# Three experts' first layers as 15 transposed products each, on a four-layer convolutional mixer

## The chip, the core and the metric

The kernel runs on one core of one Trainium2 chip. Its metric is the device time of one execution in microseconds (us): the median of several runs, with the lowest and the highest beside it. All data are 4-byte floats.

[...]

## The reference

The input `x` has 8 images of 384 channels and 32 x 32 pixels. Four layers follow, each `x = x + layer(_gn(x))`, where `_gn` is a group norm over 32 groups. The first is attention behind depthwise convolutions, the third a 7x7 depthwise convolution, the fourth a mixture of branches. The change touches the second, a mixture of four experts that all see every pixel:

```python
def _L1_conv_ref(x, gate_w, gate_b, w1, b1, w2, b2):
    ...
    scores = jax.nn.softmax(x_flat @ gate_w + gate_b, -1)
    top_v, top_i = jax.lax.top_k(scores, K)
    top_w = jax.nn.softmax(top_v, -1)
    wmap = top_w.T.reshape(K, b, h, w)
    present = (top_i[:, :, None] == jnp.arange(e)[None, None, :]).any(0)
    coef = jnp.einsum('ke,kbhw->ebhw', present.astype(x.dtype), wmap)
    hdn = jax.nn.relu(jnp.einsum('bchw,edc->ebdhw', x, w1) + b1[:, None, :, None, None])
    y = jnp.einsum('ebdhw,eod->ebohw', hdn, w2) + b2[:, None, :, None, None]
    out = jnp.einsum('ebohw,ebhw->bohw', y, coef)
    return out
```

`present` asks only whether any pixel chose an expert in a place. Where every expert is chosen somewhere in both places, `coef` is 1 everywhere, and the layer is the plain sum of four two-layer networks with 384 hidden units. The kernel computes that sum, records the gate logits beside it, and repeats from there by another path if some expert was never chosen.

## The kernel before, in words

Channels lie on the 128 partitions in three blocks (`NC` = 3); an image is 1024 pixels in the free dimension. The experts' stage, in the function `experts`, goes through the 8 images in order, each in two halves of 512 pixels (`HF`), and a half has two parts. The engines PE, ACT, DVE and POOL keep the order in which the program issues their work here (`manual_schedule`); SP's order is set by a scheduler.

First layers: for each of four experts `e` and three blocks `dc` of hidden units, three matmuls of 128 x 128 weights with 512 columns add up in one PSUM tile `ph` (line 1306), and ACT writes `relu(ph + b1)` into `hs` (line 1310). `hs` is one buffer of [block, expert, 512].

Second layers: the product of the 3 x 3 blocks of `w2` with the 3 x 2 blocks of `hs` (the half is cut again into two quarters of 256 pixels, `QF`) is made with 15 block products in place of 18. The table `PRODUCTS` gives for each which sum of weight blocks (`wsum`, made once by POOL), which sum of hidden blocks (`hs_sum`) and to which output blocks it is added or subtracted. The four experts add up in PSUM, so one product is four matmuls of 256 columns into a tile `p` (line 1217; four such tiles), and DVE adds each to its two or more places in the residual tile `r` (lines 1231 and 1233). The hidden sums (`HSUMS`, `sums`, line 1210) are made by DVE: eight for the first three experts in one operation each, eight for the fourth, and two more, for all four experts, in the middle of the products.

Between these run, by place in the loop: `normed` (ACT: the normed input `xn` of the next half, four buffers; issued at product 2), `residual` (loads of the next image's `zraw` and `x`, and the DVE sums `add_x`, line 1115; issued during the first layers), `logits` (24 small matmuls, an ACT copy and two transposes, in the first layers of an image's second half), and `next_layer`, the norm of the finished image for the third layer: `moments2` (DVE), `over_groups` (14 small matmul records, `gn_ps`), `norm2` (DVE with one power on POOL), and for each block `pass_on` (ACT scale, a DVE transpose, two POOL copies of edge rows, a store from SP). These ran after the first, third and following groups of the next image's first layers:

```python
if h == 0 and passing and k in (0, 2, 3, 4, 5, 6):
    next(passing)
...
if h == 1 and k == 3 and b + 1 < B:
    next(ahead)
if k == 9:
    sums(hs, HSUMS[:-2], slice(0, E - 1))
```

## Time and profile before

| What | Value |
|---|---|
| median of 3 runs | 3170.65 us (3167.68 to 3175.04) |
| the profiled execution's own time | 3172.27 us |
| its span in the profile | 3170.5 us |
| mean granted PE clock | 0.982 |
| experts' stage: first `ph` matmul to last `r` operation | 1731.2 to 2669 us |
| `ph` matmul records, `p` matmul records | 1152, 1920 |
| DVE `hs_sum` operations | 288 |
| POOL busy over the whole span | 253.9 us (8%) |

Times in a timeline are microseconds from the span's start: the start of a line's first operation, then the time until the last of its merged operations ends. In brackets stands the idle time of that engine before it, and what ended that. In the groups a line carries engine, operation, output and inputs with shapes, the count, the busy time and the mean of one in ns. Matmuls overlap in the pipeline, so one takes longer than the distance to the next.

### The profile page before, as it was taken

The numbers are of one execution on the slowest core, as the hardware profiler recorded it, in microseconds if no ns is written. First come the engines' busy times: TensorE is split into PE (matmuls) and PEld (weight loads), VectorE is DVE, ScalarE is ACT, GpSimd is POOL, SyncE is SP. The second block draws the span as 40 slices with busy tenths as digits, with TensorE's granted clock in tenths as the row PEclk, the third lists the DMA queues.
The fourth block names the chain that finished last, engine by engine and source line by source line (L and its number), as shares of the span: only waits on it lengthen the run. The fifth ranks groups of instructions, "written<-read, shape, count | busy, mean of one in ns | idle before, by whom it ended". The sixth has DMA issues, their size and how long they took to land.

```text
span 3170.5 us, 42235 instructions
## 1 busy us (share of the span) xinstructions
PE 3023.9 (95%) x17740; PEld 1605.6 (51%) x17740; DVE 1694.7 (53%) x2570; ACT 1190.1 (38%) x1356; POOL 253.9 (8%) x415
## 2 busy tenths in 40 slices
PE   4988999999999999999998999999999999886998
PEld 3775434343433334343433576676665666555543
DVE  6998354445444444445445464564554555447164
ACT  3554453535445353535442221212212112446510
POOL 2432000000000000000001100000000000111400
PEclk9999999999999999999999999999999999998999
DMA  6787011011101111011004021121121113867775
GB/s 222 270 280 288 33 41 65 23 62 43 60 25 60 43 43 62 23 62 43 11 25 163 20 64 40 64 64 40 64 64 49 42 44 129 332 223 241 234 226 185
DMA packets 89089, 322.84 MB, mean 102 GB/s; under 512 B 13608, under 2 KB 16000, under 8 KB 84664
## 3 DMA queue, kind: packets, MB, share of 16 engines
q1 hardware_dynamic: 64936, 251.71, 23.5%
q10 hardware_dynamic: 13776, 35.82, 3.6%
q0 software_dynamic: 10176, 32.51, 3.0%
q8 instruction: 141, 2.31, 0.3%
q14 instruction: 60, 0.49, 0.1%
HBM read 211.66 MB, written 111.68 MB: 102 GB/s over the span
## 4 chain that ended last, share of the span: by engine, by line
PE 82%; DVE 8%; DMA 6%; issue 2%; ACT 1%; POOL 1%; SPq 0%; ACTq 0%; POOLq 0%; DVEq 0%
PE ph L1306 16%; PE sc L734 15%; PE av L753 14%; PE p L1217 13%; PE sc L632 7%; PE sc L687 4%; PE sc L809 4%; DMA w<-in_w 3%; DVE stats L213 2%; DVE y L462 2%; PE ps L1783 2%; PE po L2197 1%; PE po L2200 1%; PE po L2208 1%; DVE xt L429 1%
## 5 line engine op out<-in xcount | busy, mean ns | idle before, releaser
L741 ACT ACTIVATE e<-sc 128x1024 f32<-128x1024 f32 x512 | 483.2, 1031 | 608.2 <-PE sc L734 608.1
L1306 PE MATMUL ph<-xn,w 128*128 128x512 f32 x1152 | 504.1, 596 | 3.0 <-ACT xn L315 3.0
L734 PE MATMUL sc<-qT,kT 64*128 64x512 f32 x2048 | 473.9, 602 | 0.0
L753 PE MATMUL av<-e,vT 128*64 128x512 f32 x2048 | 467.8, 599 | 0.0
L1310 ACT ACTIVATE hs<-ph,b 128x512 f32<-128x512 f32 x192 | 131.8, 686 | 705.7 <-PE ph L1306 705.4
L1306 PEld LDWEIGHTS ph<-xn,w 128*128 128x128 f32 x1152 | 218.2, 191 | 264.6 <-issue 258.6
L734 PEld LDWEIGHTS sc<-qT,kT 64*128 64x128 f32 x2048 | 186.9, 186 | 282.0 <-issue 231.1
L753 PEld LDWEIGHTS av<-e,vT 128*64 128x64 f32 x2048 | 135.6, 137 | 316.4 <-issue 316.4
L632 PE MATMUL sc<-y,pw 128*128 128x512 f32 x576 | 249.3, 594 | 0.0
L491 PE MATMUL ps<-xt,wx 64*64 64x256 f32 x3456 | 200.3, 392 | 35.2 <-DVE xt L429 20.1
L1231 DVE TENSOR_TENSOR r<-r,p 128x256 f32<-128x256 f32 x416 | 157.1, 417 | 138.9 <-PE p L1217 138.9
L769 DVE LOAD_MASK_SELECT sm<-av x64 | 0.9, 14 | 417.0 <-PE av L753 417.0
L771 DVE RECIPROCAL inv<-sm 128x512 f32<-128x512 f32 x64 | 214.6, 3353 | 2.2
L491 PEld LDWEIGHTS ps<-xt,wx 64*64 64x64 f32 x3456 | 158.8, 139 | 75.6 <-issue 38.9
L1065 PE MATMUL ps<-xt,wx 64*64 64x256 f32 (+1 forms) x2912 | 159.1, 377 | 22.6 <-ACT wx L1539 11.8
L632 PEld LDWEIGHTS sc<-y,pw 128*128 128x128 f32 x576 | 109.1, 190 | 139.7 <-issue 138.3
L1217 PE MATMUL p<-hs_sum,wsum 128*128 128x256 f32 x768 | 173.6, 379 | 0.0
L1217 PEld LDWEIGHTS p<-hs_sum,wsum 128*128 128x128 f32 x768 | 146.3, 190 | 19.5
L1210 DVE TENSOR_TENSOR hs_sum<-hs,hs_sum 128x768 f32<-128x768 f32 (+1 forms) x192 | 146.9, 779 | 4.9
L1065 PEld LDWEIGHTS ps<-xt,wx 64*64 64x64 f32 x2912 | 109.1, 138 | 70.8 <-ACT wx L1539 14.1
L687 PE MATMUL sc<-pw_v,y 128*128 128x384 f32 x384 | 128.2, 495 | 10.9 <-ACT y L315 10.9
L366 ACT COPY o<-ps 128x2048 f32<-128x2048 f32 x56 | 103.9, 1856 | 81.6 <-PE ps L491 47.4
(320 smaller groups left out, 3246.8 us busy)
## 6 DMA issues: line engine op xcount, KB each, us to landing
raw<-y SPq DMA_DIRECT2D x72, 512.0 KB
y<-raw SPq DMA_DIRECT2D x24, 1536.0 KB
x<-x SPq DMA_DIRECT2D x23, 608.0 KB
xt<-x SPq DMA_DIRECT2D x23, 608.0 KB
w<-in_w ACTq DMA_DIRECT2D x36, 384.0 KB
xn<-in_x SPq DMA_DIRECT2D x24, 512.0 KB
x<-in_x SPq DMA_DIRECT2D x16, 768.0 KB
z<-z POOLq DMA_DIRECT2D x16, 768.0 KB, 4.3
```

The source lines that it names most:

```text
L491: nc.tensor.matmul(ps[64 * d : 64 * d + 64, 2 * i + e, cc], lhsT=w[r, 12 * cc + 6 * e + 3 * d + k, :], rhs=xt0s[ct][r, 16 * d + 4 * u + 2 ...
L632: nc.tensor.matmul(ps[:, h, :], lhsT=w[:, ct, pair, :], rhs=y[:, ct, h * HF : (h + 1) * HF], start=ct == 0, stop=ct == NC - 1,)
L687: nc.tensor.matmul(ps[:, m, :C], lhsT=y[:, ct, (m0 + m) * P : (m0 + m + 1) * P], rhs=pw_v[:, ct, :], start=ct == 0, stop=ct == NC - 1,)
L734: nc.tensor.matmul(sc[:, s, :], lhsT=kTs[b][r, pair, m * P : (m + 1) * P], rhs=qTs[b][r, pair, h * HF : (h + 1) * HF], start=True, stop=True,)
L741: nc.scalar.activation(e, sc, AF.Exp, scale=1.0 if shifted else HD**-0.5)
L753: nc.tensor.matmul(av[64 * s : 64 * s + 64, :], lhsT=vTs[0][:, m, c0 : c0 + 64], rhs=e[:, s, :], start=m == 0, stop=m == N // P - 1,)
L771: nc.vector.reciprocal(inv, sm)
L1065: nc.tensor.matmul(ps[64 * d : 64 * d + 64, 2 * i + e, c % 2, images], lhsT=w[r, d * K7 + k, :], rhs=by_slot(xts[ct])[r, 16 * d + column(c ...
L1210: nc.vector.tensor_add(rows_of(o, hs, s), rows_of(i, hs, s), rows_of(j, hs, s))
L1217: nc.tensor.matmul(ps[:, :QF], lhsT=block(w)[:, e], rhs=rows_of(x, hs, e), start=e == 0, stop=e == E - 1,)
L1231: nc.vector.tensor_tensor(out=o, in0=o, in1=ps[:, :QF], op=op)
L1306: nc.tensor.matmul(ph, lhsT=w1[:, e, ct, dc * P : (dc + 1) * P], rhs=xns[b, h][:, ct, :], start=ct == 0, stop=ct == NC - 1,)
```

## The change

In all halves but the first, three of the four experts make their first layer as `w1` blocks times input by the same scheme of 15 products, transposed: what were sums of results become sums of inputs, and the reverse. POOL makes twelve sums of normed input blocks (`FORMS`, tile `forms`) for each half, shared by the three experts, and once the weight sums `w1sum`. Each product is a single matmul of 256 columns into a `p` tile (`dual`); ACT and DVE merge it at once into the hidden blocks through ten intermediate nodes, which lie in the fourth expert's part of `hs_sum`: per expert 2 ACT copies, 19 DVE operations and 3 ReLUs in place (`rectify`). The fourth expert keeps its three groups of matmuls, one ahead of each of the others (`classical`). The sums for the second layers move from DVE to POOL, one expert at a time. `next_layer`, the next image's loads and `add_x` move from the first layers to between the second layers' products (`jobs`); `xn` has two buffers.

```diff
+FORMS = (
+    (4, (1, 1), (0, 1), -1),
+    (14, 4, (2, 1), 1),
...
+DUAL = (
+    (14, ((14, "p14"),)),
+    (4, (((1, 1), "p4", 14, 1),)),
+    (13, ((1, "p13", 14, 1),)),
+    (1, (((1, 0), "p1", 1, 1),)),
+    (12, ((9, "p12", 1, 1),)),
+    (0, (((0, 0), "p0", 9, 1),)),
+    (11, ((6, "p11", 9, 1),)),
+    (3, (((0, 1), "p3", 6, 1),)),
+    (7, ((10, 6, "p7", -1),)),
+    (10, ((11, "p10"), ((0, 0), (0, 0), "p10", 1))),
+    (9, ((8, 11, "p9", -1), ((1, 0), (1, 0), 8, 1))),
+    (8, ((3, "p8", 8, 1), ((1, 1), (1, 1), 3, 1), (10, 10, 3, 1))),
+    (2, (((2, 0), "p2", 10, 1),)),
+    (6, (((0, 1), (0, 1), "p6", 1), ((2, 1), "p6", 10, 1))),
+    (5, (((1, 1), (1, 1), "p5", 1), ((2, 1), (2, 1), "p5", 1))),
+)
+NODE_AT = {n: i for i, n in enumerate((1, 9, 6, 10, 14, 11, 8, 3))}
+READY = {6: (0,), 5: (1, 2)}
...
-                xn = xns[b, h] = wq.tile([P, NC, HF], FP, tag="xn", name="xn", bufs=4)
+                xn = xns[b, h] = wq.tile([P, NC, HF], FP, tag="xn", name="xn", bufs=2)
...
+            forms = wq.tile([P, len(FORMS), QF], FP, name="forms")
+            w1sum = wq.tile([P, len(wslot) - 2, R15, P], FP, name="w1sum")
...
+            def make_forms(xn):
+                for o, i, j, sign in FORMS:
+                    i, j = (form_of(v, xn) for v in (i, j))
+                    nc.gpsimd.tensor_tensor(
+                        out=forms[:, fslot[o]], in0=i, in1=j,
+                        op=ALU.add if sign > 0 else ALU.subtract,
+                    )
+
+            def rectify(hs, e, m):
+                affine(hs[:, m, e], hs[:, m, e], 1.0, b1[:, e, m : m + 1], AF.Relu)
+
+            def dual(hs, e, xn):
...
+                for n, ops in DUAL:
+                    ps = got[f"p{n}"] = ep.tile([P, HF], FP, tag="p", name="p")
+                    nc.tensor.matmul(
+                        ps[:, :QF], lhsT=block1(PRODUCTS[n][0])[:, e], rhs=form_of(n, xn),
+                        start=True, stop=True,
+                    )
+                    for o, i, *more in ops:
+                        if not more:
+                            nc.scalar.copy(at(o), at(i))
+                            continue
+                        j, sign = more
+                        nc.vector.tensor_tensor(
+                            out=at(o), in0=at(i), in1=at(j), op=ALU.add if sign > 0 else ALU.subtract
+                        )
+                    for m in READY.get(n, ()):
+                        rectify(hs, e, m)
...
-            def sums(hs, some, s):
+            def sums(hs, some, s, eng=nc.vector):
...
+                    nxt = (b, 1) if h == 0 else (b + 1, 0)
+                    if i == 2 and nxt[0] < B:
+                        normed(*nxt)
...
-                        sums(hs, HSUMS[-2:], slice(0, E))
+                        sums(hs, HSUMS[-2:], slice(0, E), nc.gpsimd)
+                    if i == 4 and nxt[0] < B:
+                        make_forms(xns[nxt])
+                    for job in jobs.get(i, ()):
+                        job()
...
+                    next(gating, None)
+                    for e in range(R15):
+                        classical(hs, R15, e, xn)
+                        dual(hs, e, xn)
                         next(gating, None)
+                        if e == R15 - 1:
+                            sums(hs, HSUMS[:-2], slice(R15, E), nc.gpsimd)
+                        sums(hs, HSUMS[:-2], slice(e, e + 1), nc.gpsimd)
...
+                jobs = {}
+                if h == 0:
+                    if passing:
+                        for i in (0, 1, 2, 5, 7, 9):
+                            jobs[i] = (lambda p=passing: next(p),)
+                    if b + 1 < B:
+                        jobs[10] = (lambda b=b: fetch_next(b + 1),)
+                elif b + 1 < B:
+                    jobs[0] = (lambda b=b: next(ahead[b + 1]),)
+                products(b, h, hs, jobs)
```

More of the change, by code (lines that the diff above doesn't have):

```diff
@@ L112 @@
 )
+R15 = 3
+FORMS = (
+    (4, (1, 1), (0, 1), -1),
+    (14, 4, (2, 1), 1),
+    (13, (2, 0), 14, -1),
+    (1, (0, 0), (1, 0), -1),
+    (0, (0, 0), (2, 0), -1),
+    (11, (0, 1), (2, 0), -1),
+    (3, (2, 1), (0, 1), -1),
+    (10, (1, 0), 14, -1),
+    (8, (0, 1), (1, 0), -1),
+    (2, (0, 0), (0, 1), -1),
+    (6, (2, 1), (2, 0), -1),
+    (5, (1, 1), (1, 0), -1),
+)
+PLAIN = {7: (0, 1), 9: (1, 0), 12: (2, 0)}
+DUAL = (
[15 rows of a table added]
+)
+NODE_AT = {n: i for i, n in enumerate((1, 9, 6, 10, 14, 11, 8, 3))}
+READY = {6: (0,), 5: (1, 2)}
 def img(a):
@@ L1187, in experts @@
             hs_sum = ew.tile([P, len(HSUMS) - 2, E, QF], FP, name="hs_sum")
+            fslot = {n: i for i, (n, *_) in enumerate(FORMS)}
             lg = ew.tile([P, NT, E], FP, name="lg")
@@ L1198, in experts, with block1, sum_weights @@
                 )
+            w1slot = {n: i for i, n in enumerate(n for n in wslot if n not in (8, 9))}
+            def block1(n):
+                n = {8: (1, 1), 9: (2, 0)}.get(n, n)
+                if isinstance(n, tuple):
+                    return w1[:, :R15, n[0], n[1] * P : (n[1] + 1) * P]
+                return w1sum[:, w1slot[n]]
+            def sum_weights():
+                for o, i, sign, j in WSUMS:
+                    first8 = o == 8 and i != 8
+                    nc.gpsimd.tensor_tensor(
+                        out=block1(5 if first8 else o), in0=block1(5 if i == 8 else i), in1=block1(j),
+                        op=ALU.add if sign > 0 else ALU.subtract,
+                    )
@@ new lines, in form_of @@
+            def form_of(n, xn):
+                n = PLAIN.get(n, n) if isinstance(n, int) else n
+                if isinstance(n, tuple):
+                    return xn[:, n[0], n[1] * QF : (n[1] + 1) * QF]
+                return forms[:, fslot[n]]
+            def make_forms(xn):
+                for o, i, j, sign in FORMS:
+                    i, j = (form_of(v, xn) for v in (i, j))
+                    nc.gpsimd.tensor_tensor(
+                        out=forms[:, fslot[o]], in0=i, in1=j,
+                        op=ALU.add if sign > 0 else ALU.subtract,
+                    )
@@ new lines, in rectify, with at @@
+            def rectify(hs, e, m):
+                affine(hs[:, m, e], hs[:, m, e], 1.0, b1[:, e, m : m + 1], AF.Relu)
+            def dual(hs, e, xn):
+                got = {}
+                def at(n):
+                    if isinstance(n, str):
+                        return got[n][:, :QF]
+                    if isinstance(n, tuple):
+                        return hs[:, n[0], e, n[1] * QF : (n[1] + 1) * QF]
+                    return hs_sum[:, NODE_AT[n], E - 1]
+                for n, ops in DUAL:
[3 more added lines that the diff above has]
+                        start=True, stop=True,
+                    )
+                    for o, i, *more in ops:
[5 more added lines that the diff above has]
+                            out=at(o), in0=at(i), in1=at(j), op=ALU.add if sign > 0 else ALU.subtract
+                        )
+                    for m in READY.get(n, ()):
+                        rectify(hs, e, m)
@@ L1199, in experts, with classical @@
+            def classical(hs, e, dc, xn):
+                ph = eh.tile([P, HF], FP, tag="h", name="ph", bufs=3)
+                for ct in range(NC):
+                    nc.tensor.matmul(
+                        ph, lhsT=w1[:, e, ct, dc * P : (dc + 1) * P], rhs=xn[:, ct, :],
+                        start=ct == 0, stop=ct == NC - 1,
+                    )
+                nc.scalar.activation(hs[:, dc, e], ph, AF.Relu, bias=b1[:, e, dc : dc + 1])
             nc.vector.tensor_reduce(badd, b2, AX.X, ALU.add)
@@ L1206, in rows_of, with products @@
                 return hs_sum[:, hslot[n], s]
-            def sums(hs, some, s):
+            def sums(hs, some, s, eng=nc.vector):
                 for o, i, j in some:
-                    nc.vector.tensor_add(rows_of(o, hs, s), rows_of(i, hs, s), rows_of(j, hs, s))
-            def products(b, h, hs):
+                    eng.tensor_add(rows_of(o, hs, s), rows_of(i, hs, s), rows_of(j, hs, s))
+            def products(b, h, hs, jobs):
                 r, begun = rs[b], set()
@@ L1220, in products @@
                         )
-                    if i == 2:
-                        if h == 0:
-                            normed(b, 1)
-                        elif b + 1 < B:
-                            normed(b + 1, 0)
+                    nxt = (b, 1) if h == 0 else (b + 1, 0)
+                    if i == 2 and nxt[0] < B:
+                        normed(*nxt)
                     for sign, m, n in outs:
@@ L1297, in logits, with fetch_next @@
                 yield
-            ahead, passing = None, None
+            ahead, passing = {}, None
+            def fetch_next(b):
+                ahead[b] = residual(b)
+                next(ahead[b])
             for b, h in product(range(B), range(2)):
                 hs = ew.tile([P, NC, E, HF], FP, tag="hs", name="hs")
-                gating = logits(b)
-                for k, (e, dc) in enumerate(TODO):
-                    ph = eh.tile([P, HF], FP, tag="h", name="ph", bufs=3)
-                    for ct in range(NC):
-                        nc.tensor.matmul(
-                            ph, lhsT=w1[:, e, ct, dc * P : (dc + 1) * P], rhs=xns[b, h][:, ct, :],
-                            start=ct == 0, stop=ct == NC - 1,
-                        )
-                    nc.scalar.activation(hs[:, dc, e], ph, AF.Relu, bias=b1[:, e, dc : dc + 1])
-                    if h == 0 and passing and k in (0, 2, 3, 4, 5, 6):
-                        next(passing)
-                    if h == 0 and k == 9 and b + 1 < B:
-                        ahead = residual(b + 1)
-                        next(ahead)
-                    if h == 1 and k in (0, 1, 2, 4):
-                        next(gating, None)
-                    if h == 1 and k == 3 and b + 1 < B:
-                        next(ahead)
-                    if k == 9:
-                        sums(hs, HSUMS[:-2], slice(0, E - 1))
-                sums(hs, HSUMS[:-2], slice(E - 1, E))
+                xn = xns[b, h]
+                gating = logits(b) if h else iter(())
+                if (b, h) == (0, 0):
+                    for k, (e, dc) in enumerate(TODO):
+                        classical(hs, e, dc, xn)
+                        if k == 9:
+                            sums(hs, HSUMS[:-2], slice(0, E - 1))
+                    sums(hs, HSUMS[:-2], slice(E - 1, E))
+                    sum_weights()
+                else:
+                    next(gating, None)
+                    for e in range(R15):
+                        classical(hs, R15, e, xn)
+                        dual(hs, e, xn)
+                        next(gating, None)
+                        if e == R15 - 1:
+                            sums(hs, HSUMS[:-2], slice(R15, E), nc.gpsimd)
+                        sums(hs, HSUMS[:-2], slice(e, e + 1), nc.gpsimd)
                 if (b, h) == (B - 1, 1):
@@ L1325, in experts @@
                     begin_layer2(B - 1, er)
-                products(b, h, hs)
+                jobs = {}
[8 more added lines that the diff above has]
+                products(b, h, hs, jobs)
                 if h == 1:
```

## The prediction, made before the changed kernel ran

> **What bounds the kernel now.** I read the page first: busy shares, then the chain that ended last. TensorE is busy 95% of the span and the chain lies on it for 82%; the two lines to be changed, `ph` (first layers) and `p` (second layers), hold 16% and 13%.

> ```profile
> PE 3023.9 (95%) x17740; PEld 1605.6 (51%) x17740; DVE 1694.7 (53%) x2570; ACT 1190.1 (38%) x1356; POOL 253.9 (8%) x415
> PE 82%; DVE 8%; DMA 6%; issue 2%; ACT 1%; POOL 1%; SPq 0%; ACTq 0%; POOLq 0%; DVEq 0%
> ```

> Then the timeline of one half image, for prices. A 4-byte matmul shows as two records. From 2099.62 to 2115.07 are 36 records, 0.429 each: 0.859 per matmul of 512 columns. The next 24 take 5.18 to 2120.25: 0.431 per matmul of 256. TensorE stops nowhere: half an image is 36 x 0.859 + 60 x 0.431 = 56.8, plus 1.5 for gate logits or 1.9 for the norm's group matmuls; sixteen halves make 936, and the stage runs from 1731.2 to 2667.9.

> ```profile
> 2099.62 15.61 PE L1306 MATMUL ph<-xn,w 128*128 128x512 f32 x36
> 2115.07 5.34 PE L1217 MATMUL p<-hs,w 128*128 128x256 f32 x24
> 2117.12 2.14 DVE L1210 TENSOR_TENSOR hs_sum<-hs,hs_sum 128x256 f32<-128x256 f32 x5
> 2120.25 3.62 PE L1217 MATMUL p<-hs,wsum 128*128 128x256 f32 x16
> 2133.88 1.80 DVE L1231 TENSOR_TENSOR r<-r,p 128x256 f32<-128x256 f32 x5
> ```

> VectorE: independent 256-element operations follow each other every 0.345 ((1.80-0.42)/4); one that needs the last takes about 0.45. So everything the change adds on other engines is free only while TensorE need not wait, and I look for those waits.

> **The saving.** In 15 of 16 halves (the first stays), three experts' 27 wide matmuls (23.2) become 45 narrow ones (19.4): 3.8 less per half, **57.0** in all. The bound from below is the same figure: no other TensorE work goes.

> **(a) The tail of the transposed products.** Each expert needs 19 vector operations for 15 products of 0.431. For the first eight operations VectorE keeps step. The last six products carry eleven. The ninth product's operation ends 4.5 after the expert's first matmul started (9 x 0.431, 0.2 until it can be read, 0.42); eight more at 0.40 bring block (0,1), and a ReLU over 512 elements (0.80, the mean of the group `xn<-r,tb,s`) makes it 8.5. PE ends the last expert at 6.47 and, after experts 0 and 1 of product P0, wants that block at 7.33: with the hand-overs a wait of 1.4, and nothing else to run. Three of the eleven read two SBUF tiles; the next view says what GpSimd does to them.

> ```profile
> 1738.32 1.26 POOL L1196 TENSOR_TENSOR wsum<-w 128x512 f32<-128x512 f32 x1 [4.87 <-DMA r<-z]
> 1738.42 1.18 DVE L1200 TENSOR_TENSOR badd<-badd,zn_t 128x3 f32<-128x3 f32 x1
> 1739.52 0.17 DVE L1201 TENSOR_TENSOR ref<-gm,gmy 128x24 f32<-128x24 f32 x1
> 2657.52 0.75 DVE L1231 TENSOR_TENSOR r<-r,p 128x256 f32<-128x256 f32 x2 [1.30 <-PE p L1217]
> 2657.57 0.75 POOL L1522 TENSOR_TENSOR w<-w 128x84 f32<-128x84 f32 x2 [0.60 <-PE p L1217]
> ```

> A three-element sum took 1.18, not 0.17: it ended with the GpSimd sum beside it. The two `r<-r,p` beside GpSimd lost nothing; one of their inputs is in PSUM. So only the three operations with two SBUF inputs should wait, each for up to one GpSimd operation. GpSimd then is in sums all through the last expert. Its 256-element sum is in no row; bounds are 0.397 (84 elements) and 1.263 (512), linear between them 0.745. Three waits add 2.2 to 2.4: the tail is 3.7. Fifteen halves: **55** (21 without the lock).

> ```profile
> L1196 POOL TENSOR_TENSOR wsum<-w 128x512 f32<-128x512 f32 x5 | 6.3, 1263 | 4.9 <-DMA r<-z 4.9
> L1522 POOL TENSOR_TENSOR w<-w 128x84 f32<-128x84 f32 x28 | 10.5, 397 | 144.8 <-DMA w<-in_w 144.2 <-PE p L1217 0.6
> ```

> [...]

> **(b) Buffers.** Four PSUM buffers serve products. An expert's three ReLUs (0.7 to 0.8 each, ending about 10.1 after it began) sit on ScalarE ahead of the next expert's 0.69 ReLU and the copy of its product 14 (0.47, the row of `lt`, also 256 from PSUM); that buffer is free at 11.2, and PE wants it at 9.05 + 4 x 0.431 = 10.8. With later tails this is 0.6 to 1.2 per half: **18** (9 without the lock).

> **(c) The norm.** Image b-1's moments now stand on VectorE behind P0's two results, and the group matmuls on PE right behind P1. Seven halves.

> ```profile
> 2083.81 1.28 DVE L213 BATCH_NORM_STATS2 gn_bs<-r 128x6 f32<-128x512 f32 x2
> ...
> 2088.55 0.16 DVE L276 TENSOR_TENSOR dq<-dq,gn_mv 128x3 f32<-128x3 f32 x1
> 2090.34 1.62 PE L267 MATMUL gn_ps<-dq,gmatA 128*128 128x2 f32 x14
> ```

> Moments take 4.9 (2083.81 to 2088.71). Before, PE had two more 2.58 groups to run meanwhile. Now: 0.2 until P0 can be read, 0.87 for its results, 4.9, less the 1.72 of P1: PE stands 4.3, and P2 to P14 stand behind it. `dq` is three operations with two SBUF inputs, so up to 2.2 more. I take 6.6 x 7 = **46** (31 without). The power step on GpSimd (0.85) queues behind the sums, but its results are wanted only by P5's turn: nothing. The six edge copies now stand behind twelve forms; the third transpose waits for the first's store (two `x2` buffers), some 0.3, at most 3 per image; in the range.

> **(d) The residual sum.** In the other halves `add_x` stands on VectorE behind P0's results:

> ```profile
> 2151.05 2.48 DVE L1115 SCALAR_TENSOR_TENSOR r<-r,zn_s,xr 128x1024 f32<-128x1024 f32 x2
> 2156.13 1.28 DVE L1115 SCALAR_TENSOR_TENSOR r<-r,zn_s,xr 128x1024 f32<-128x1024 f32 x1 [2.59 <-DMA xr<-in_x]
> ```

> 6.36 with its DMA wait. P1 to P4 fill the four buffers in 6.9; P1's are free after 0.2 + 0.87 + 6.36 + 0.87 = 8.3: PE waits 1.4. All three operations read two SBUF tiles while GpSimd sums: up to 2.2 more, and they hold GpSimd up. I take 2.7 x 7 = **19** (10 without).

> **(e) The clock.** A pause costs more than itself:

> ```profile
> 2679.77 0.92 PE L267 MATMUL gn_ps<-dq,gmatA 128*128 128x2 f32 x6 [2.86 <-DVE dq L276]
> 2670.00:2680.00 10.00, 7.00 (x210) 6.51 (x202) 6.66 (x20) 1.24 (x1) 1.05 (x3) 1.00 0.67 150
> 2680.00:2690.00 10.00, 10.00 (x262) 9.46 (x265) 5.40 (x9) 5.10 (x7) 1.94 (x5) 0.83 0.17 65
> ```

> The last two lines are windows; the column behind the last bracket is the granted clock. After a wait of 2.86, the next 10 us had 0.83: 1.7 lost. Seven norm waits: **12**. Tail waits of 3.7 are about that long too: between 0 and 15 x 1.7 = 25; I take the middle, **13**. [...]

> **(f) The first half.** VectorE's sums for the second layers now meet GpSimd's 13 new weight sums (384 elements, by the same line 1.0 each); waits of up to one each push P0's results back: **6**, once. The weight sums end under the half's 26 of products; without that cover the first transposed product would wait up to 13, once.

> **At nothing.** The ten sums leave VectorE (about 13 per half), which had the time. `xn` has two buffers, not four: each is rewritten from P2 on, when its readers (first layers, logits) are done. The eight `r2mem` stores (7.1 on SP's queue, 2083.92 on) move to P0; nothing queued behind them is wanted before P7. The next image's loads go from the first layer to P10, still 29 ahead of their use. At the stage's start SP issues `r` before `xr` and the first weights; before, all of these were out by 1681, fifty ahead of PE's start at 1731.

> **Sum.** -57 + 55 + 18 + 46 + 19 + 12 + 13 + 6 = +112. The profiled execution took 3172.27 (span 3170.5 and 1.77 around it), 1.6 above the median of the runs. 3172.3 + 112 - 1.6 = **3283**.

> **Rivals.** *No lock cost* (0.17): GpSimd and VectorE share without waiting. For it: GpSimd's own rows beside VectorE hardly lengthen. Then -57 + 21 + 9 + 31 + 10 + 12 = +26: **3197**, 3175 to 3225 with (e) and the transposes' wait.

> *GpSimd becomes the bound* (0.10). Per half it has 32 sums and 12 forms of 256 elements and two sums of 1024 (by the line 2.3). From expert 1's sums, at 22.5 into the half, come 36 short operations and one long before P13 can start: 22.5 + 36 x 0.75 + 2.3 and some 6 behind VectorE's two-input operations make 58. PE is at P13 after 27.1 + 22.4 and waits of 7.6: 57. So 0.745 is about the point from which it decides; at 0.90 each half gains 36 x 0.155 = 5.6, 15 halves some 80: **3363**. Against it: the line through 84 and 512 elements has little room to err.

> *Faster* (0.07): VectorE ends an expert as fast as PE, because the eleven late operations overlap instead of following each other. Then only the norm wait stays: -57 + 31 + 12 = -14, **3157**. It decides where all other waits of a half are under 0.95 (14 / 15). Against it: the five `hs_sum` took 2.14 in a row, not 1.8.

> *The work is done, but its gain and waits cancel* (0.04): the unlocked waits, with the tail near zero; within 6 of 3171.

> **How the numbers follow.** The first case has 0.62 and, by (a) 2.5 to 4.2 per half, (c) 5.5 to 7.1, (e) without or with all tails, and the transposes' wait, its own range 3240 to 3325. The range 3185 to 3360 takes it whole, most of the unlocked case and half of the GpSimd case: some 0.8. A change of about 0.2% (6.3 us) is what this measurement can tell from none. Faster by more 0.07, within 0.04, slower 0.89.

> **What would show it.** `ph` 1152 records down to 342 (72 + 15 x 18), and 1350 new records of 256 columns; the group matmuls waiting for `dq` seven times, 4 us at least; the first products waiting some 1.4 (no lock) or 3.7 (lock) for ReLU; `hs<-hs,hs_sum` at 0.42 or well above; GpSimd's 256-element operations near 0.75; the granted clock below 1.0 in the stage. Wrong, if those waits are under 1, or if the operations with a PSUM input are stretched by GpSimd too: 13 more waits per expert would then go past 3360.

## The result, and the profile after

The changed kernel takes 3263.76 us (median of 4 runs, 3259.38 to 3269.79) where the kernel before takes 3172.85 (3167.68 to 3175.44): a ratio of 1.029, 95% interval 1.0268 to 1.0312. It is slower by about 91 us. The forecast was 3283, with 3185 to 3360. The side and the mechanism were right; several sizes were not, and their errors partly cancelled.

The page after, busy shares and the chain that ended last (PE is TensorE, DVE VectorE, ACT ScalarE, POOL GpSimd):

```profile
PE 3039.0 (93%) x18280; PEld 1724.5 (53%) x18280; DVE 1851.4 (57%) x3153; ACT 1215.5 (37%) x1446; POOL 837.5 (26%) x1120
PE 68%; DVE 14%; DMA 6%; ACT 4%; POOL 3%; issue 3%; SPq 0%; ACTq 0%; DVEq 0%; POOLq 0%
```

The chain lay on PE for 82% of the span and now does for 68%; what left it went to DVE, ACT and POOL. Where that is, a window over the experts' stage shows (first `ph` to the last `p`; columns: length, busy time of PE, PEld, DVE, ACT and POOL, then the granted clock). First before, then after:

```profile
1731.23:2667.84 936.61, 936.61 (x3378) 602.83 (x3378) 505.52 (x974) 196.99 (x276) 37.88 (x71) 1.00 0.19 59
```

```profile
1733.36:2760.73 1027.37, 947.68 (x3918) 722.79 (x3918) 662.62 (x1557) 223.06 (x366) 622.57 (x776) 0.95 0.17 54
```

The stage is 90.8 longer, of the span's 97.5. (It begins 2.1 later, and 4.6 comes behind it; I followed neither.) PE, which never stood still, is now idle for 79.7. And although its matmuls should take less time, its busy time rose by 11.1 at a mean clock of 0.95. The waits behind the 79.7, in PE's waits within the stage (us in all, times, longest):

```profile
PE gn_ps L304 <- DVE dq L313: 29.1, 7, 4.7
PE p L1326 <- ACT hs L352: 28.2, 15, 1.9
PE p L1326 <- DVE r L1340: 11.4, 5, 8.1
PE p L1284 <- ACT hs_sum L1290: 9.3, 23, 0.5
...
PE p L1326 <- POOL hs_sum L1319: 0.9, 4, 0.3
```

They are the forecast's places: norm (c), tail (a), the first half (f, the 8.1) with the residual sum (d, the other 3.3), buffers (b), and GpSimd, which nearly never ends last. The timeline of one half shows a tail and a norm:

```profile
2148.65 0.50 DVE L1293 TENSOR_TENSOR hs<-hs,hs_sum 128x256 f32<-128x256 f32 x1
...
2148.67 1.13 PE L1326 MATMUL p<-hs,w 128*128 128x256 f32 x4
2148.83 2.46 POOL L1319 TENSOR_TENSOR hs_sum<-hs 128x256 f32<-128x256 f32 x3
2149.07 0.94 DVE L1293 TENSOR_TENSOR hs_sum<-hs_sum 128x256 f32<-128x256 f32 x1
...
2151.68 2.86 PE L1326 MATMUL p<-hs,w 128*128 128x256 f32 x12 [1.88 <-ACT hs L352]
...
2158.19 0.69 DVE L312 TENSOR_TENSOR dq<-dq 128x3 f32<-128x3 f32 x1
...
2159.22 3.12 PE L304 MATMUL gn_ps<-dq,gmatA 128*128 128x2 f32 x14 [4.68 <-DVE dq L313]
...
2162.20 3.76 PE L1326 MATMUL p<-hs,w 128*128 128x256 f32 x8
...
2165.75 4.58 PE L1326 MATMUL p<-hs,wsum 128*128 128x256 f32 x16
```

PE waits 1.88 for the last ReLUs and 4.68 for `dq`. Then the same 14 group matmuls that took 1.62 before take 3.12, and eight records of `p` take 3.76 where eight take 1.89 elsewhere (at 2183.98, for one). Windows of 2 us say why; the clock stands behind the last bracket:

```profile
2156.00:2158.00 2.00, 0.00 (x0) 0.00 (x0) 1.90 (x6) 0.00 (x0) 1.92 (x3) 0.86 0.00 0
2158.00:2160.00 2.00, 0.78 (x4) 0.81 (x5) 1.72 (x5) 0.00 (x0) 1.84 (x4) 0.50 0.00 0
...
2166.00:2168.00 2.00, 2.00 (x6) 1.60 (x6) 1.27 (x6) 0.00 (x0) 0.65 (x1) 0.58 0.04 8
2168.00:2170.00 2.00, 2.00 (x11) 1.76 (x10) 1.40 (x3) 1.04 (x1) 1.84 (x4) 1.00 0.00 0
```

From about 2157.4 to 2167.7 the clock is at half: three steps of 3.41 us. The clock's record changes in such steps throughout, and in this stage 32 of them are at half where the kernel before has one (in both, one lies at the stage's start).

### The profile page after: what moved, and what is told of

It reads as the page before. It is cut to its first block, busy times and chain, and to the rows that moved or that the text cites. A ratio compares the mean times of both kernels' runs of the same rounds, so it can differ in the third digit from the quotient of the medians.

```text
span 3268.0 us, 45156 instructions
## 1 busy us (share of the span) xinstructions
PE 3039.0 (93%) x18280; PEld 1724.5 (53%) x18280; DVE 1851.4 (57%) x3153; ACT 1215.5 (37%) x1446; POOL 837.5 (26%) x1120
## 3 DMA queue, kind: packets, MB, share of 16 engines
q1 hardware_dynamic: 64936, 251.71, 22.7%
## 4 chain that ended last, share of the span: by engine, by line
PE 68%; DVE 14%; DMA 6%; ACT 4%; POOL 3%; issue 3%; SPq 0%; ACTq 0%; DVEq 0%; POOLq 0%
PE sc L771 14%; PE av L790 14%; PE p L1326 9%; PE sc L669 7%; PE p L1284 5%; PE sc L724 4%; PE sc L846 4%; PE ph L1302 3%; DVE hs L1293 2%; DVE stats L250 2%; DVE y L499 2%; DMA w<-in_w 2%; ACT hs L352 2%; POOL hs_sum L1319 2%; DMA r<-r 1%
## 5 line engine op out<-in xcount | busy, mean ns | idle before, releaser
L1319 POOL TENSOR_TENSOR hs_sum<-hs,hs_sum 128x256 f32<-128x256 f32 (+1 forms) x332 | 304.6, 925 | 22.2 <-PE p L1326 1.9
L820 POOL DMA_DIRECT2D att<-att x45 | 23.7, 531 | 981.1 <-DVE att L815 981.1
L1319 POOL TENSOR_TENSOR hs_sum<-hs 128x256 f32<-128x256 f32 x180 | 138.8, 798 | 313.3 <-ACT hs L352 288.2
L528 PEld LDWEIGHTS ps<-xt,wx 64*64 64x64 f32 x3456 | 157.3, 138 | 76.2 <-issue 37.9
L1293 DVE TENSOR_TENSOR hs<-p,hs_sum 128x256 f32<-128x256 f32 x270 | 114.3, 423 | 130.0 <-ACT hs_sum L1290 110.9
L1284 PE MATMUL p<-forms,w 128*128 128x256 f32 x630 | 166.2, 380 | 0.0
L1302 PE MATMUL ph<-xn,w 128*128 128x512 f32 x342 | 157.3, 602 | 3.0 <-ACT xn L352 3.0
L352 ACT ACTIVATE hs<-hs,b 128x512 f32<-128x512 f32 x135 | 89.8, 717 | 162.3 <-DVE hs L1293 162.3
```

Of the source, the lines that this page charges most:

```text
L528: nc.tensor.matmul(ps[64 * d : 64 * d + 64, 2 * i + e, cc], lhsT=w[r, 12 * cc + 6 * e + 3 * d + k, :], rhs=xt0s[ct][r, 16 * d + 4 * u + 2 ...
L1284: nc.tensor.matmul(ps[:, :QF], lhsT=block1(PRODUCTS[n][0])[:, e], rhs=form_of(n, xn), start=True, stop=True,)
L1293: nc.vector.tensor_tensor(out=at(o), in0=at(i), in1=at(j), op=ALU.add if sign > 0 else ALU.subtract)
L1302: nc.tensor.matmul(ph, lhsT=w1[:, e, ct, dc * P : (dc + 1) * P], rhs=xn[:, ct, :], start=ct == 0, stop=ct == NC - 1,)
L1319: eng.tensor_add(rows_of(o, hs, s), rows_of(i, hs, s), rows_of(j, hs, s))
```

## Experiments

This table holds the stage of every run but sums_on_vector, in us. "Beyond" is PE's busy time over that of the same products in a stage whose clock stayed up (894.6, six_moves; for the two kernels without transposed products 940.2, six_no_transposed). "Clock" is the sum over windows of 3.41 us of busy time x (1 - granted clock); with windows set exactly on the record's steps it comes out up to 1.1 higher. In "beyond" lies also the first part of each wait, since the record of a 256-column matmul lasts longer (0.38) than the distance to the next (0.22) and so covers it.

| kernel | stage | PE idle | idle work added | beyond | clock |
|---|---|---|---|---|---|
| changed kernel | 1027.4 | 79.7 | 0 | 53.1 | 47.9 |
| norm_filled | 1003.7 | 55.5 | 30.2 | 23.5 | 18.4 |
| both_filled | 1000.5 | 37.1 | 56.0 | 12.7 | 6.8 |
| norm_later | 972.5 | 58.6 | 0 | 19.3 | 11.6 |
| tail_covered | 1020.8 | 85.7 | 0 | 40.5 | 34.4 |
| no_sums | 994.0 | 68.1 | 0 | 31.3 | 28.0 |
| no_transposed | 1008.3 | 44.0 | 0 | 24.1 | 26.3 |
| four_moves | 957.4 | 44.3 | 0 | 18.5 | 6.5 |
| five_moves | 951.9 | 36.2 | 0 | 21.1 | 17.2 |
| six_moves | 917.2 | 22.7 | 0 | 0 | 1.5 |
| six_no_transposed | 952.0 | 11.8 | 0 | 0 | 1.5 |

**norm_filled: is it the clock?** The wait stays, but PE is given something to do in it.

```diff
...
+                        jobs[1] = (lambda xn=xn: keep_busy(10, xn),) + jobs[1]
```

> The changed kernel with ten products of 256 columns put on TensorE ahead of the norm's group matmuls in seven halves; they write a spare PSUM buffer that nobody reads. They cover the wait for dq (4.68 where it was looked at) with idle work: the waiting time stays, 10 x 0.431 = 4.31 of it as work. Theory A (a pause of TensorE costs its own length and, behind it, one to three stretches of 3.4 us at half clock): the clock stays up behind the norm, so 7 halves x 3.4 to 5.1 lost = 24 to 36 come back: 3228 to 3240. Rival B (a pause costs its own length only, and the other 68 us of the stage are the narrow products themselves, costing more than 0.431): nothing comes back, 3260 to 3268.

Measured: 3243.32, ratio 1.0221 (1.0204 to 1.0238), some 20 below the changed kernel. PE's timeline at the same place:

```profile
2145.32 2.86 PE L1326 MATMUL p<-hs,w 128*128 128x256 f32 x12 [1.87 <-ACT hs L352]
2148.01 4.48 PE L1419 MATMUL ph<-xn,w 128*128 128x256 f32 x20
2152.87 1.69 PE L304 MATMUL gn_ps<-dq,gmatA 128*128 128x2 f32 x14 [0.38 <-DVE dq L313]
2154.42 1.97 PE L1326 MATMUL p<-hs,w 128*128 128x256 f32 x8
```

The group matmuls are back at 1.69 and the eight records behind them at 1.97. The same wait, filled with work that nobody reads, makes the kernel faster: rival B falls. In "beyond" 29.6 came back, within A's 24 to 36. The time fell by less, because the wait for `r` rose from 11.4 to 16.9: of the seven halves with the residual sum the clock now stays up behind the tail in four, not one, and PE comes to that sum earlier.

**norm_later: the wait and its clock together.** The fifteen products of a half are called P0 to P14. Moments stay at P0; the group matmuls go behind P4.

```diff
-                    if i == 8:
+                    if i == 6:
                         sums(hs, HSUMS[-2:], slice(0, E), nc.gpsimd)
...
-                        for i in (0, 1, 2, 5, 7, 9):
+                        for i in (0, 4, 4, 7, 9, 11):
...
```

> The changed kernel with the norm's group matmuls and power step moved from P1 and P2 to P4 (ahead of the next half's forms), the passing-on from P5, P7, P9 to P7, P9, P11, and GpSimd's last two sums from P8 to P6. Moments still stand behind P0's results and have P1 to P4 (6.9 us of TensorE) as their cover. Theory A: the wait (4.2 x 7 = 29) and the clock lost behind it (24 to 36) both go: minus 53 to 65, 3199 to 3211. Rival B: only the wait goes, 3232 to 3238. Rival C (the wait moves to the products' results, since VectorE is as late as before): under 10 us gained.

Measured: 3208.81, ratio 1.0117 (1.01 to 1.0134): minus 55, as theory A has it. The seven waits for `dq` are gone from the stage, and the clock's loss falls from 47.9 to 11.6.

**tail_covered: does the tail cost what it shows?**

```diff
+                for some in ((0, 1, 3), (2,)):
+                    for ps, (w, x, _) in zip(pair, PRODUCTS):
+                        for e in some:
+                            nc.tensor.matmul(
...
```

> The changed kernel with the second layers' first two products woven: P0 and P1 first take experts 0, 1 and 3 (six matmuls, 2.6 us), then expert 2 of both, whose last ReLU is what P0 waited for 1.88 us in 15 halves. The order of everything else stays. Theory A: 15 x 1.7 of waiting = 25, and one stretch of half clock (1.7) in 8 to 11 halves = 14 to 19: minus 39 to 44, 3220 to 3225. Rival B: the waiting alone, minus 25, 3239. Rival C: P0's results come 1.3 later, so moments and the norm's wait lengthen by as much in seven halves (plus 9 on either).

Measured: 3259.82, ratio 1.0264 (1.0247 to 1.0281): 4 less, which this measurement can hardly tell from nothing. All three expectations were too low. PE's timeline, again tail and norm:

```profile
2146.41 1.56 PE L1327 MATMUL p<-hs,w 128*128 128x256 f32 x6
...
2148.34 2.44 PE L1327 MATMUL p<-hs,w 128*128 128x256 f32 x10 [0.36 <-DVE hs L1293]
...
2156.76 3.12 PE L304 MATMUL gn_ps<-dq,gmatA 128*128 128x2 f32 x14 [5.98 <-DVE dq L313]
```

The tail's 28.2 became 5.5, and PE waits so much longer at the next place: `dq` 29.1 to 41.9, `r` 11.4 to 28.2. VectorE ends these two, in nearly every half, and it does not end earlier because PE did. So the tail alone was hardly on the path.

**both_filled: the second halves of the images.** As norm_filled, and four such matmuls ahead of P0's third expert.

> As norm_filled, and four more products of 256 columns (1.72) put on TensorE ahead of P0's third expert, in fifteen halves, so that the tail's wait (1.88) is nearly all covered with idle work too. Theory A (in the second half of an image the stretch at half clock behind the tail lies beside the residual sum on VectorE, which ends last there): the clock stays up, but P4 waits for VectorE's results by what the clock gives back: 3236 to 3246, as norm_filled (3243). Rival (clock and waits add up): nine stretches of half clock fewer, 1.7 each, 3228.

Measured: 3238.85, ratio 1.0207 (1.019 to 1.0225): theory A. The second half of an image in the changed kernel, then here:

```profile
2092.64 6.23 PE L1326 MATMUL p<-hs,w 128*128 128x256 f32 x20 [1.89 <-ACT hs L352]
...
2102.91 1.32 PE L1326 MATMUL p<-hs_sum,w 128*128 128x256 f32 x5 [0.59 <-DVE r L1340]
```

```profile
2081.66 4.58 PE L1328 MATMUL p<-hs,w 128*128 128x256 f32 x20 [0.16 <-ACT hs L352]
2091.82 3.69 PE L1328 MATMUL p<-hs_sum,w 128*128 128x256 f32 x16 [2.12 <-DVE r L1342]
```

Twenty records fall from 6.23 to 4.58, 1.65 given back by the clock, and the next wait rises from 0.59 to 2.12, by 1.53. Here half a clock lay beside a wait and cost nearly nothing.

**no_sums: what GpSimd's sums cost VectorE.** They are left out of fifteen halves.

```diff
...
-                        if e == R15 - 1:
-                            sums(hs, HSUMS[:-2], slice(R15, E), nc.gpsimd)
-                        sums(hs, HSUMS[:-2], slice(e, e + 1), nc.gpsimd)
```

> The changed kernel without GpSimd's ten sums of the ReLU outputs in fifteen halves: the second layers' products read the sums that the first half left in their place. GpSimd keeps the twelve forms per half, weight sums and the norm's small steps. It takes away what the shared access of GpSimd and VectorE costs at the tail, in the norm and in the residual sum. Lock theory as far as the trace shows it: at the tail 0.08 + 0.08 + 0.52 (the three two-SBUF operations at 0.50, 0.50, 0.94 against 0.42), so 15 x 0.7 = 10; the norm 0.5 x 7 = 4; the residual sum 3 x 0.33 x 7 = 7 at most; with shorter pauses losing less clock, up to 15 more: minus 15 to 35, 3229 to 3249. Lock as forecast before (tail 2.3, norm 2.3, residual sum 1.3): minus 60 or more. No lock: within 6 of 3264.

Measured: 3229.31, ratio 1.0176 (1.0159 to 1.0193): minus 34. The groups by form (the mean in ns stands behind the comma), changed kernel and then no_sums:

```profile
L1293 DVE TENSOR_TENSOR hs<-p,hs_sum 128x256 f32<-128x256 f32 x270 | 114.3, 423 | 130.0 <-ACT hs_sum L1290 110.9 <-PE p L1284 0.5
...
L1293 DVE TENSOR_TENSOR hs<-hs,hs_sum 128x256 f32<-128x256 f32 x90 | 45.4, 505 | 3.1
...
L1152 DVE SCALAR_TENSOR_TENSOR r<-r,zn_s,xr 128x1024 f32<-128x1024 f32 x21 | 33.2, 1609 | 13.1 <-DMA xr<-in_x 13.1
...
L1293 DVE TENSOR_TENSOR hs_sum<-hs_sum 128x256 f32<-128x256 f32 x45 | 26.6, 592 | 0.0
```

```profile
L1293 DVE TENSOR_TENSOR hs<-p,hs_sum 128x256 f32<-128x256 f32 x270 | 114.3, 423 | 128.6 <-ACT hs_sum L1290 109.5 <-PE p L1284 0.5
...
L1293 DVE TENSOR_TENSOR hs<-hs,hs_sum 128x256 f32<-128x256 f32 x90 | 38.2, 425 | 3.1
...
L1152 DVE SCALAR_TENSOR_TENSOR r<-r,zn_s,xr 128x1024 f32<-128x1024 f32 x21 | 26.3, 1279 | 17.5 <-DMA xr<-in_x 17.5
...
L1293 DVE TENSOR_TENSOR hs_sum<-hs_sum 128x256 f32<-128x256 f32 x45 | 18.8, 418 | 0.0
```

Operations with two SBUF inputs are stretched by GpSimd's sums (0.505 against 0.425, 1.609 against 1.279); those with one input in PSUM are not (0.423 both times). The tail's wait falls from 1.88 to 1.27, the buffers' from 9.3 to 3.7. Idle time gives 11.6 of the stage's 33.4 and busy time 21.8, nearly all of it clock: none of the fifteen pauses of 1.27 is followed by a step at half, where 11 of the 1.88 were.

**no_transposed and sums_on_vector: one part undone.**

```diff
...
-                        dual(hs, e, xn)
+                        for dc in range(NC):
+                            classical(hs, e, dc, xn)
```

> One part undone: the changed kernel with all twelve first-layer blocks as wide products again, without the transposed products, their nodes, forms and weight sums; the sums by GpSimd, the norm among the second layers' products and the loads stay as changed. Theory A: the norm's wait (4.2 to 4.7) and three stretches of half clock (5.1) in seven halves are the price of the moved norm alone, 65 to 70, and the residual sum costs some 0.6 to 1.4 in seven halves, 4 to 10: 3172 + 69 to 80 = 3241 to 3252. The transposed products then cost the changed kernel some 12 to 23 net, though they save 57 on TensorE. Rival B (without the tail the clock holds, pauses cost their own length): 3172 + 34 to 43 = 3206 to 3215.

Measured: 3247.94, ratio 1.0231 (1.0215 to 1.0246): theory A. What the change moved among the second layers' products costs 75 without any transposed product, most of it through the norm: `dq` is waited for 35.6 in 7, the residual sum for 8.3 in 7, and the clock takes 26.3. The transposed products, with all that belongs to them, add only some 16 to that.

```diff
...
-                        sums(hs, HSUMS[:-2], slice(e, e + 1), nc.gpsimd)
+                        sums(hs, HSUMS[:-2], slice(e, e + 1))
```

> One part undone: the changed kernel with the ten sums of the ReLU outputs on VectorE again. Lock theory alone: as without the sums, 3229, since VectorE has 43% of the span free. Order theory: the last two experts' sums (16 operations, 5.5 to 6.5) stand on VectorE ahead of P0's results, so the norm's wait and the residual sum's waits grow by about that in 14 halves, 77 to 91, with up to one more stretch of half clock each (24), and each expert's sums (2.8) push the next expert's nodes back: 3310 to 3370.

Measured: 3417.63, ratio 1.0779 (1.0762 to 1.0795). The order theory, and more than it asked: PE waits 66.1 in 7 for `dq`, 50.2 in 16 for `r` and 60.2 in 30 for the nodes (`hs`, line 1293), and the stage's clock is 0.91. VectorE's free 43% is not where these sums stand in its order. At these points of the order GpSimd, with its price, is the better place for them.

**four_moves, five_moves, six_moves: taking away what is late.** The first three edits together (norm_later, tail_covered, the first half's weight sums behind P8), and the residual sum split:

```diff
+                    if ct == 1:
+                        yield
...
-                    sum_weights()
...
+                if (b, h) == (0, 0):
+                    jobs[8] = (sum_weights,)
```

> The changed kernel with four moves at once: the norm later (as norm_later), P0 and P1 woven (as tail_covered), the residual sum's third operation put behind P1's results instead of P0's (its DMA wait of 2.1 then lies beside P1's results), and the first half's 13 weight sums put on GpSimd behind P8's turn, out of VectorE's sums. From norm_later (3209): tail 28 of waiting less the 5.5 that weaving leaves = -23; P4's wait in the first half -8; the residual sum's waits -9; eight of the ten stretches at half clock, 1.7 each, -14. Theory A (each pause costs itself and its clock, and with all late elements moved none is left): 3155, 3145 to 3165, faster than the kernel before. Rival (as with tail_covered, what is taken at one place is waited for at the next, GpSimd's sums among them): 3190 or more.

Measured: 3194.41, ratio 1.0067 (1.0053 to 1.0081): the rival's side. The first half's 8.2 is gone and the tail's 28.2 is 5.5; but P13 and P14 now wait 13.8 for GpSimd's sums, which had cost 0.9, and `dq` is waited for again, 5.7 in 7.

```diff
+                        relu = classical(hs, R15, e, xn)
+                        dual(hs, e, xn, relu)
```

> As four_moves, and the ReLU of the fourth expert's block on ScalarE is put behind the copy of product 14 instead of ahead of it, in each of 45 experts; that copy frees the PSUM buffer for which the transposed products wait (0.42 each, 10.0 in 24). Theory A: these waits go, with 0.2 each for the pipeline to fill again: 10 to 15 below four_moves, 3140 to 3145. Rival: the copy is held by the three ReLUs of the expert before, not by the fourth expert's: under 3 gained.

Measured: 3187.7, ratio 1.0047 (1.0033 to 1.006): 7 less, between the two expectations. The wait for the copy fell from 10.1 to 1.2, but GpSimd's rose and became the largest:

```profile
PE p L1340 <- POOL hs_sum L1325: 17.2, 11, 2.8
```

The clock's loss rose again, to 17.2. Six steps at half follow six of the seven longest waits for GpSimd, 2.2 and more ahead of P13. In four halves half a clock now follows a mere 0.7 of waiting for `dq`, together with the group matmuls of two columns behind it.

```diff
-                    if i == 6:
-                        sums(hs, HSUMS[-2:], slice(0, E), nc.gpsimd)
+                    if i == 8:
+                        sums(hs, HSUMS[-2:], slice(0, E))
...
-                        for i in (0, 4, 4, 7, 9, 11):
+                        for i in (0, 5, 5, 7, 9, 11):
```

> As five_moves, with what its trace shows as late next moved too: the last two sums (two of 1024 elements, 4.8 on GpSimd, for which P13 waits 17.2 us in 11) on VectorE behind P8; the norm's group matmuls, power step and the next half's forms behind P5 instead of P4 (they waited 0.7 seven times); the residual sum's second and third operation both behind P1's results (P5 waited 0.9 seven times). Theory A (GpSimd's queue of sums and forms is the bound by now, and each late element moved takes its clock along): waits 17 + 5 + 6 go, and some eleven stretches of half clock at 1.7 each, 18: minus 40 to 46, 3142 to 3148. Rival: VectorE, with 2.6 more per half and GpSimd's forms beside it, is late instead, or the third residual operation waits for its DMA: 3165 or more.

Measured: 3154.85, ratio 0.9939 (0.9926 to 0.9953): the fastest of all, below the kernel before by 0.6%, and between theory A and the rival. The window over the stage and PE's waits in it:

```profile
1728.10:2645.30 917.20, 894.55 (x3918) 689.41 (x3918) 693.83 (x1589) 223.62 (x366) 572.98 (x744) 1.00 0.20 60
```

```profile
PE p L1339 <- POOL hs_sum L1324: 9.9, 7, 1.4
PE p L1339 <- DVE r L1353: 6.4, 7, 0.9
PE p L1332 <- DVE hs L1296: 5.5, 15, 0.4
```

The clock is 1.00, although some waits are 1.4 long. The time stays 7 above theory A's 3142 to 3148: P13's wait is gone, but in seven halves P5, the first product that reads sums, now waits up to 1.4 for GpSimd, 9.9 in all.

> The moves of six_moves (apart from the one that concerns product 14) with the three experts' first layers as wide products, without nodes, forms and weight sums: what the transposed products are worth once nothing waits. Theory A: TensorE is busy all through the stage and the time is the kernel before's, 3168 to 3180; six_moves minus this one is then what is left of the 57 saved. Rival: moved norm and residual sum still cost something without the transposed products, 3190 or more.

Measured: 3188.7, ratio 1.0048 (1.0033 to 1.0061), between the two. The 11.8 of waiting left in it are the residual sum's (14 times). Run beside it, six_moves is 34 faster: that is what the transposed products are worth here, once what they make late is moved.

## Why the prediction was right, and where it was not

The forecast's sum was +112, the stage's increase is 90.8. Step by step, from the table: 936.6 less 42.0 saved (936.6 - 894.6), plus 79.7 idle, plus 53.1 beyond, is 1027.4.

- **The saving** was put at 57 and is 42.0, or 45.6 against six_no_transposed. The rate of 0.431 held. The forecast took the stage to be products alone; 11 to 15 of the saving did not arrive. In six_no_transposed 14 waits leave 3.6 of busy time over before, 0.26 each, so by estimate the 29 of six_moves would explain about 7; the rest stays open. (The forecast's prices for sixteen halves before add up to 934, not 936. At the stage's start 3.7 us run at half clock, which is worth the other 1.8.)
- **(a) The tail:** 28.2 measured, 55 forecast. The part without GpSimd's sums was right (1.4; 1.27 in no_sums). The part that the forecast calls the lock was mis-sized: three operations were to wait 2.3 together, by an estimate from one row of the kernel before (1.18 in place of 0.17), and lost 0.08, 0.08 and 0.52.
- **(b) Buffers:** 9.3 against 18; 3.7 against 9 without GpSimd's sums.
- **(c) The norm:** 29.1 against 46; without GpSimd's sums beside it 31 were forecast, and no_sums shows 29.1. With them the forecast had 2.2 more a wait, and it is 0.5: `dq` is stretched (0.69 for one operation of 0.16), and where the clock was up behind the tail, in three halves, the wait is 4.7 against 4.2 in no_sums. In the other four a step at half clock lies over the products ahead of the group matmuls, and the wait is 3.6 to 4.3.
- **(d) The residual sum:** 3.3 against 19, for PE had lost time to the tail and the clock before it came there. Where the tail's wait is taken away the sum shows: 20.0 in tail_covered (28.2 less the first half's 8.2). Where the clock is given back it shows too, as 2.12 in place of 0.59 in both_filled.
- **(e) The clock:** forecast 25, measured 46 over the kernel before. The forecast took 1.7 per pause, from a wait of 2.86. A norm wait with the group matmuls behind it halves the clock for three steps in four halves and for two in three, 5.1 or 3.4 each; and of the 15 tail pauses, though half as long as forecast, 11 cost a step. This is the term that was too small.
- **(f) The first half:** 8.1 against 6, with two more steps at half clock behind it.

So the waits, forecast at 144 with the first half, came to 79, and the clock with what waits hide came to 53 in place of 25. With a saving 15 too large, the errors cancelled in part, down to 21; that the sum came this near is in part luck. The terms were also added as if each pause lay on the path alone. Tail, clock, residual sum and norm wait for the same VectorE one after the other in each half: tail_covered removed 23 of waiting at the tail and won 4.

**The rivals.** "No lock cost" (3197) fell by no_sums: without the sums 34 come back, so VectorE's operations beside them do cost something (0.505 against 0.425 each), though the forecast gave it 86. "GpSimd becomes the bound" (3363) did not happen: the 480 sums of 256 elements took 0.77 on average, near the 0.745 forecast, and cost 0.9 of waiting. But it stood next in the row, and was the largest wait in four_moves and five_moves. The faster case's 3157 was reached only in six_moves, with moves that the change does not have.

How much one operation lost varies. In the changed kernel 69 of the nodes' 135 operations with two SBUF inputs ran beside a GpSimd operation: 46 took 0.49 to 0.56, 21 took 0.94 to 0.99 and 2 lost nothing, against 0.41 to 0.43 for those that ran beside none. GpSimd's sums last 0.77, so most lost far less than the whole GpSimd operation that the forecast allowed each. With the PSUM input as the first operand nothing was lost: the 264 that ran beside a GpSimd operation and the 186 that ran beside none all took 0.41 to 0.43. GpSimd in its turn lost time: its 339 sums of 256 hidden elements beside no two-SBUF operation of VectorE took 0.71 to 0.74, and of the 141 beside one 75 took longer, up to 1.76.

## What to carry to other kernels

Price a pause of TensorE with the clock behind it: here moving the norm out of 29 us of waiting gave back 55 (norm_later), and idle matmuls in the same wait made the kernel faster. A wait that the trace shows is only worth what the next wait behind it leaves: before counting on its removal, ask which engine ends last further on and whether it starts any earlier. Work moved off a loaded engine should go where its queue is free at that point, and the steps that wait for it should stand as many products later as it lasts.
